# A four-layer graph network kernel: one transfer sums two neighbouring slots, a front's steps have fixed homes, 16 tile buffers, a third of the slots summed

## The chip, the core and the metric

The kernel runs on one core of a Trainium2 chip. A core has a matrix engine (PE), a vector engine (DVE), a scalar engine (ACT), a general engine (POOL), a sequencer for transfers (SP) and 16 DMA engines that they share. The time is device microseconds of one execution; lower is better.

## The reference, cut to what matters

64 batches of 256 nodes with 128 features go through four layers, each of the form x = x + layer(relu(layernorm(x))), all with one 256 x 256 matrix adj. The first three are a gated network of five steps, a polynomial in adj, and one product with adj. The last is attention over all pairs of nodes:

```python
W1, W2 = (W[:, :F], W[:, F:])                     # W is adj here
s1 = jnp.einsum('bkf,ef->bke', x, W1)
s2 = jnp.einsum('bkf,ef->bke', x, W2)
pre = s1[:, :, None, :] + s2[:, None, :, :] + b_lin
h = jnp.where(pre >= 0, pre, ALPHA * pre)         # b x 256 x 256 x 256
e = jnp.einsum('bije,e->bij', h, a) + bias
attn = jax.nn.softmax(e, axis=2)
out = jax.nn.sigmoid(jnp.einsum('bij,bjf->bif', attn, x))
```

The tensor h has 256 values for each of 64 x 256 x 256 pairs of nodes, about a thousand million in all, and each goes through a comparison and a weighted sum over the last axis. That is most of the work.

## The kernel before, in words

Batches are taken in pairs, 32 in all. For each pair a **front** (`front`, L505 on) computes layers 0 to 2 and the small operands of layer 3; then the attention scores are made in **slots**, 64 for each pair, 2048 in all. A slot stands for 8 rows i of the score matrix, four row groups by two batches (or by two halves).

The 256 features of a slot are split in two parts of 128, sorted by the sign of their weight, so that a part is one **tile** of 128 partitions x 2048 values (`t[:, g, b, :]`, 1 MiB). A tile needs only min(s1, s2) or relu(s1 - s2); the linear rest of the leaky relu is computed apart (`lin`). Part 0 is made by DVE in one instruction (L956), part 1 by ACT in eight (L964), and POOL makes either part in eight (L970). PE then **scores** the tile: `score` (L1032 on, its matmuls at L1044) multiplies it by a window of signs, so that the sum over 128 features lands in the right row of a PSUM bank.

Some slots are **joined** (`JOINED`, L896, a share of 3 in 10, not in the last 96 slots). For them POOL makes the second part in the same min form as the first, and a DMA issued from POOL adds the one tile onto the other (`add_pair`, L990, `accum_op=OP.add`). PE then scores one tile instead of two. The addend tile is free again when the transfer has landed.

There are 14 tile buffers; a producer takes the one that is free first. `MOST` (L889) bounds how many tiles of one engine may wait to be scored.

**What sets the order.** The order of the instructions on every engine is written out when the kernel is built. The loop at the end keeps a clock for each engine, and `ran` adds an assumed duration for every instruction (2.2 us for a DVE tile, 0.873 for a quarter tile of POOL, and for a transfer `ISSUE, ADDED, LANDED` at L29: time on POOL, time between two landings, time from issue to landing). Whichever engine's clock is least behind takes what is ready: the tails and fronts first, then transfers, scores and bank fills, then tiles. `part_of` decides whether POOL makes part 0, 1 or 2. So the assumed durations decide how many tiles fall to each engine; on the chip each engine runs its list in order and waits on semaphores.

A front is a chain of steps in fixed order (`yield engine, since`), paced so that it is finished when its pair's slots come up. Its intermediate tensors (h, mT, rh, d, hT, x1, x2 ...) come from rotating pools: one pool of 12 buffers (`SHORT`), one of 4 for hT, one of 3 for x1 and x2. The first pair's two batches run apart (`alone`) and borrow two tile buffers each. The normalisation in a front uses small POOL operations (L408, L409, L489) between DVE's statistics and ACT's activation (L493). Inputs, the rows for the tail and the outputs are moved by SP's queue.

Of the kernel before, what the change touches and what calls it, by code (L numbers as in the profile page):

```python
# [8 lines left out]
F32 = mybir.dt.float32  # L9
AF = mybir.ActivationFunctionType  # L10
OP = mybir.AluOpType
# [13 lines left out]
SHARE = (3, 10)  # L25
# [3 lines left out]
ISSUE, ADDED, LANDED, SLACK = 0.93, 5.9, 7.0, 0.3  # L29
# [3 lines left out]
def kernel(  # L33
# [65 lines left out]
    tiles = [[relu_pool.tile([P, 4, NB, N], F32, name=f"rl{k}", bufs=1), 0.0] for k in range(14)]  # L99
    scratch = tiles[0][0].rearrange("p g b n -> p (g b n)")  # L100
# [60 lines left out]
    def load_x(p):  # L161
        if p >= NPAIR:
            return
        XIN[p] = work.tile([P, NB, NC, D], F32, name="xin", bufs=2)
        for b in range(NB):
            nc.sync.dma_start(XIN[p][:, b], x[p * NB + b].rearrange("(c p) d -> p c d", p=P))
# [6 lines left out]
    place = scratch[:, 0:N].bitcast(mybir.dt.int32)  # L173
# [9 lines left out]
    def load_raw(w):  # L183
        raw = work.tile([P, 2 * D], F32, name="w_raw", tag="short", bufs=12)
        nc.sync.dma_start(raw[:, :w.shape[1]], w)
        return raw
# [6 lines left out]
    th_raw = scratch[:, N:N + 5 * D].rearrange("p (k o) -> p k o", k=5)  # L193
# [36 lines left out]
    def first_constants():  # L230

        for c in range(NC):
            yield PE, 6.0, 1
            b = take()
            for k in range(NC):
                nc.tensor.transpose(b[0][:, k * P:(k + 1) * P], adj_n[:, k, c * P:(c + 1) * P], ident)
            t = ran(PE, 0.4, 6.0, b[1])
            yield DVE, t
            nc.vector.tensor_copy(adj_t[:, c, :], b[0][:, 0:N])
            t = ran(DVE, 0.35, t)  # L240
            spare.append([b[0], t])
        SET_UP.add("adj")
        sums = [raws[0][:, :D]]
        yield DVE, 6.5
        for raw in raws[1:4]:
            sums.append(work.tile([P, D], F32, name="w_sum", tag="short", bufs=12))
            nc.vector.tensor_add(sums[-1], raw[:, :D], raw[:, D:])
        t = ran(DVE, 0.6, 6.5)
        yield PE, t, 1
        b = take()  # L250
        for k, src in enumerate(sums):
            nc.tensor.transpose(b[0][:, k * P:(k + 1) * P], src, ident)
        t = ran(PE, 0.7, t, b[1])
        yield DVE, t
        nc.vector.tensor_copy(wts[:, 0:4].rearrange("p k o -> p (k o)"), b[0])
        nc.vector.tensor_sub(w34, w3t, w4t)
        t = ran(DVE, 0.85, t)
        spare.append([b[0], t])
        yield PE, 7.0, 1
        b = take()  # L260
        nc.tensor.transpose(b[0][:, 0:P], raws[4][:, :D], ident)
        t = ran(PE, 0.25, 7.0, b[1])
        yield DVE, t
        nc.vector.tensor_scalar(u5t, b[0][:, 0:P], 0.5, None, op0=OP.mult)
        t = ran(DVE, 0.25, t)
        spare.append([b[0], t])
        nc.vector.tensor_add(gate_b[:, 0:1], braw[:, 0:1], braw[:, 3:4])
        nc.vector.tensor_add(gate_b[:, 1:2], braw[:, 1:2], braw[:, 3:4])
        nc.vector.tensor_add(gate_b[:, 2:3], braw[:, 2:3], braw[:, 4:5])
        nc.vector.tensor_scalar(gate_b[:, 0:2], gate_b[:, 0:2], 0.5, None, op0=OP.mult)  # L270
        nc.vector.tensor_scalar(bh_n, bh, -1.0, None, op0=OP.mult)
        ran(DVE, 0.3)
        SET_UP.add("first")

    def other_constants():
# [31 lines left out]
        placed = work.tile([P, N], F32, name="placed", tag="short", bufs=12)  # L307
        nc.vector.tensor_copy(placed, place)
        nc.vector.tensor_copy(number, feature)
        before = work.tile([P, P], F32, name="before", tag="short", bufs=12)  # L310
        nc.vector.tensor_scalar(before, placed[:, 0:P], number[:, 0:1], None, op0=OP.is_gt)
        ones = work.tile([P, P], F32, name="ones", tag="short", bufs=12)
# [23 lines left out]
        among = work.tile([P, P], F32, name="among", tag="short", bufs=12)  # L336
# [10 lines left out]
        moved_to = work.tile([P, NE, NE, P], F32, name="moved_to", tag="short", bufs=12)  # L347
# [3 lines left out]
        adj_s = work.tile([P, NE, N], F32, name="adj_s", tag="short", bufs=12)  # L351
# [107 lines left out]
    def feat(name, **kw):  # L459
        return work.tile([P, NB, N], F32, name=name, **kw)  # L460

    def tok(name, **kw):
        return work.tile([P, NB, NC, D], F32, name=name, **kw)
# [3 lines left out]

    SHORT = dict(tag="short", bufs=12)

# [29 lines left out]
    def front(p, batches):  # L499
# [17 lines left out]
        def feature(name, **kw):  # L517
            return part().unsqueeze(1) if alone else feat(name, **(kw or SHORT))

        def token(name, **kw):  # L520
            return part().rearrange("p (b c d) -> p b c d", b=1, c=NC) if alone else tok(name, **(kw or SHORT))

# [14 lines left out]
        def copied(name, bank, t, **kw):  # L537

            c = feature(name, **kw)
            nc.scalar.copy(c, seen(bank))  # L540
            t = ran(ACT, COPY[nb], t)
            spare.append([bank[0], t])
            return c, t
# [10 lines left out]
        hT, t_hT = copied("hT", b, t, bufs=4)  # L554
        for step in range(STEPS):
# [5 lines left out]
            mT, t_m = copied("mT", b, t)  # L561
# [25 lines left out]
            rh = feature("rh")  # L587
# [23 lines left out]
            d = feature("d")  # L611
# [18 lines left out]
            hT_new = feature("hT", bufs=4)  # L630
# [15 lines left out]
        x1 = token("x1", tag="x12", bufs=3)  # L646
# [12 lines left out]
        c1T, t_c = copied("c1T", b, t)  # L659
# [5 lines left out]
        hT, t = copied("hT", b, t, bufs=4)  # L665
# [10 lines left out]
        c2T, t = copied("c2T", b, t)  # L676
# [12 lines left out]
        x2 = token("x2", tag="x12", bufs=3)  # L689
# [18 lines left out]
        yT, t = copied("yT", b, t)  # L708
# [12 lines left out]
        sq = token("sq")  # L721
# [27 lines left out]
        hT, t_hT = copied("hT", b, t, bufs=4)  # L749
# [78 lines left out]
    def tail(u, pe, since, own=range(NB)):  # L828
# [10 lines left out]
        sc = feat("sc", **SHORT)[:, 0:nb]  # L839
# [16 lines left out]
        wT = tok("wT", **SHORT)[:, 0:nb]  # L856
# [32 lines left out]
    MOST = {DVE: 8, ACT: 3, POOL: 4}  # L889
# [6 lines left out]
    JOINED = [n for n in range(NSLOT - ALONE) if (n + 1) * SHARE[0] // SHARE[1] > n * SHARE[0] // SHARE[1]]  # L896
# [4 lines left out]
    adding = [0.0]  # L901

# [32 lines left out]

    def work_on_tile(e):
        if e not in begun:
            k = part_of(e)
            tiles.sort(key=lambda t: t[1])
            begun[e] = [slot(k), k, *tiles.pop(0), 0]  # L940
            following[k] += 1
            held[e] += 1
            if k < 2:
                READY[where(begun[e][0])[0]]["left"][k] -= 1
# [39 lines left out]
    def pair_ready():  # L984

        return min(((max(x[0] for x in both.values()), n) for n, both in pairs.items() if len(both) == 2), default=None)

    def add_pair(n):
        (since, t, e), (since_z, z, e_z) = pairs[n][0], pairs.pop(n)[2]
        nc.gpsimd.dma_start(out=t.rearrange("p g b n -> p (g b n)"), in_=z.rearrange("p g b n -> p (g b n)"), accum_op=OP.add)  # L990
        issued = ran(POOL, ISSUE, since, since_z)
        done = adding[0] = max(adding[0] + ADDED, issued + LANDED)
        held[e] -= 1
        held[e_z] -= 1
        tiles.append([z, done])
        made.append((done, n, 2, t, None))
# [179 lines left out]
```

## Time and profile before

| what | value |
|---|---|
| median of 3 runs | 4719.98 us (4719.92 to 4722.61) |
| profiled execution | 4720.04 us, span 4718.2 us |
| granted PE clock | 0.999 |
| transfers that sum tiles | 585, 1024 KB each, median 8.1 us from issue to landing |
| software queue q0 | 613.45 MB, 64.9% of the 16 DMA engines' span |
| tiles made: DVE, ACT, POOL | 1775, 1235, 1086 |

How to read it: the profile's page gives busy time by engine and the costliest groups of instructions. A group's line has the source line, engine, operation, output <- inputs, shapes, count, then busy time in us and mean duration in ns, then the idle time of the engine just before these instructions and what ended it. Instructions of PE, ACT and POOL overlap with the next of the same engine, so a mean duration is longer than the step from one start to the next. PEld is PE's loading of weights.

### The profile page before, as it was taken

The page shows a single profiled execution, that of the slowest core. Times are in us where ns is not written, and L with a number is a line of the kernel's source. Part 1 is how long each engine was busy: PE and PEld are TensorE (multiplying, and loading weights), DVE is VectorE, ACT ScalarE, POOL GpSimd, SP SyncE. Part 2 cuts the span into 40 slices and gives each one's busy share as a digit, 9 for nine tenths or more (in the row PEclk, how much of TensorE's full clock was granted, in tenths as well). Part 3 has the DMA queues.
Part 4 walks back from the last instruction along what each step waited for, and adds up shares of the span by engine and source line. Part 5 has one row for each costly group of instructions (what it writes and reads, how often), then busy time and mean ns, then how long its engine had stood idle before and what let it go on. Part 6 is the DMA issues. An engine that isn't in the chain of part 4 may idle for free.

```text
span 4718.2 us, 133077 instructions
## 1 busy us (share of the span) xinstructions
PE 4693.0 (99%) x51711; PEld 1724.1 (37%) x51711; DVE 4638.2 (98%) x3664; ACT 4615.2 (98%) x12059; POOL 4565.5 (97%) x9776
## 2 busy tenths in 40 slices
PE   9999999999999999999999999999999999999999
PEld 4333333333333333333333333333333333333332
DVE  5999999999999999999999999999999999999999
ACT  5999999999999999999999999999999999999999
POOL 2999999999999999999999999999999999999998
PEclk9999999999999999999999999999999999999999
DMA  1767777777777777777777777777777777777720
GB/s 33 148 139 153 147 144 157 145 148 147 148 150 147 142 152 149 147 147 146 150 146 148 148 151 143 150 153 150 145 144 147 149 153 144 146 145 148 153 61 5
DMA packets 129378, 656.97 MB, mean 139 GB/s; under 512 B 14696, under 2 KB 49896, under 8 KB 53864
## 3 DMA queue, kind: packets, MB, share of 16 engines
q0 software_dynamic: 84240, 613.45, 64.9%
q1 hardware_dynamic: 43784, 35.01, 2.5%
q8 instruction: 404, 6.62, 0.5%
q14 instruction: 230, 1.88, 0.1%
q10 hardware_dynamic: 720, 0.00, 0.0%
HBM read 26.48 MB, written 8.52 MB: 7 GB/s over the span
## 4 chain that ended last, share of the span: by engine, by line
PE 80%; DVE 10%; POOL 4%; issue 2%; DMA 2%; ACT 2%; SPq 0%; POOLq 0%; DVEq 0%; ACTq 0%
PE bank L1044 52%; PE bank L414 25%; DVE rl L956 8%; POOL rl L970 3%; PE bank L447 2%; DMA rl<-rl 2%; ACT rl L964 1%; PE bank L439 1%; POOL rl L990 0%; DVE bank L627 0%; DVE d L623 0%; DVE hT L631 0%; DVE rh L588 0%; DVE stats L484 0%; DVE bank L836 0%
## 5 line engine op out<-in xcount | busy, mean ns | idle before, releaser
L956 DVE TENSOR_TENSOR rl<-s1a,bank 128x2048 f32<-128x2048 f32 x1775 | 3964.5, 2277 | 8.7 <-DMA rl<-rl 4.9
L964 ACT ACTIVATE rl<-bank,s1b 128x256 f32<-128x256 f32 x9880 | 3938.3, 727 | 5.2 <-PE bank L1044 3.5
L970 POOL TENSOR_SCALAR rl<-s2n,s1b 128x256 f32<-128x256 f32 x6504 | 3101.4, 790 | 18.7 <-ACT s1b L802 7.5
L1044 PE MATMUL bank<-rl,win_n 128*32 128x512 f32 x18208 | 2258.9, 593 | 7.0 <-DMA rl<-rl 4.9
L1044 PE MATMUL bank<-rl,win 128*32 128x512 f32 x9880 | 1303.8, 593 | 0.0
L970 POOL TENSOR_SCALAR rl<-s2c,s1a 128x256 f32<-128x256 f32 x2184 | 1054.3, 741 | 2.4
L1044 PEld LDWEIGHTS bank<-rl,win_n 128*32 128x32 f32 x18208 | 586.0, 110 | 1210.5 <-issue 1022.9
L990 POOL DMA_DIRECT2D rl<-rl x585 | 617.4, 1068 | 3.8 <-DVE rl L956 1.5
L1044 PEld LDWEIGHTS bank<-rl,win 128*32 128x32 f32 x9880 | 319.9, 110 | 633.8 <-issue 509.2
L414 PE MATMUL bank<-mT,wts 128*32 128x512 f32 x2480 | 322.8, 592 | 0.0
L414 PE MATMUL bank<-adj_t,h 128*32 128x256 f32 x4960 | 297.5, 380 | 2.4 <-ACT h L642 2.4
L414 PEld LDWEIGHTS bank<-adj_t,h 128*32 128x32 f32 x4960 | 159.8, 110 | 163.0 <-issue 48.0
L493 ACT ACTIVATE h<-x,mv 128x128 f32<-128x128 f32 x376 | 166.7, 617 | 11.1 <-POOL mv L489 10.3
L414 PE MATMUL bank<-mT,w 128*32 128x512 f32 x1240 | 161.5, 592 | 0.8 <-ACT bank L584 0.8
L414 PE MATMUL bank<-hT,wts 128*32 128x512 f32 x1240 | 161.8, 593 | 0.0
L414 PE MATMUL bank<-rh,u5t 128*32 128x512 f32 x1240 | 161.4, 592 | 0.0
L584 ACT ACTIVATE bank<-bank,gate_b 128x512 f32<-128x512 f32 (+1 forms) x165 | 138.0, 836 | 20.1 <-PE bank L414 17.4
L414 PEld LDWEIGHTS bank<-mT,wts 128*32 128x32 f32 x2480 | 80.4, 110 | 185.9 <-issue 137.0
L607 ACT ACTIVATE bank<-bank,gate_b 128x512 f32<-128x512 f32 (+1 forms) x165 | 138.4, 839 | 9.7 <-PE bank L414 9.5
L409 POOL TENSOR_TENSOR mv<-mv,minus_half 128x4 f32<-128x4 f32 (+1 forms) x132 | 133.8, 1014 | 11.0
L540 ACT COPY mT<-bank 128x512 f32<-128x512 f32 x155 | 123.9, 800 | 12.7 <-PE bank L414 11.9
L620 ACT ACTIVATE bank<-bank,gate_b 128x512 f32<-128x512 f32 x155 | 131.1, 845 | 3.1 <-PE bank L414 3.1
(207 smaller groups left out, 3164.4 us busy)
## 6 DMA issues: line engine op xcount, KB each, us to landing
rl<-rl POOLq DMA_DIRECT2D x585, 1024.0 KB, 8.1
rows<-row SPq DMA_DIRECT2D x31, 512.0 KB
xin<-in_x_dram SPq DMA_DIRECT2D x64, 128.0 KB
out_dram<-o SPq DMA_DIRECT2D x63, 128.0 KB
row<-quarter SPq DMA_DIRECT2D x62, 2.0 KB
rows<-row SPq DMA_DIRECT2D x2, 256.0 KB
w_raw<-in_L_gnn_w_w_dram SPq DMA_DIRECT2D x3, 128.0 KB
rl<-in_L_gnn_Theta_dram SPq DMA_DIRECT2D x1, 320.0 KB
```

Of the source, the lines that this page charges most:

```text
L409: nc.gpsimd.tensor_tensor(t, t, minus_half[:, 0:t.shape[1]], op=OP.pow)
L414: nc.tensor.matmul(o[g:g + 32], w[:, g:g + 32], t, start=start, stop=stop, skip_group_check=True)
L493: nc.scalar.activation(h[:, k, :], s[:, k, :], AF.Relu, bias=mv[:, k, 0:1], scale=mv[:, k, 1:2])
L540: nc.scalar.copy(c, seen(bank))
L584: nc.scalar.activation(seen(r), seen(pr), AF.Tanh, bias=br, scale=0.5)
L607: nc.scalar.activation(seen(pr), seen(pr), AF.Tanh, bias=bz, scale=0.5)
L620: nc.scalar.activation(seen(pv), seen(pv), AF.Tanh, bias=bh_n, scale=-1.0)
L956: nc.vector.tensor_tensor(t, rows.to_broadcast(whole), ops["s2a"].unsqueeze(1).to_broadcast(whole), op=OP.min)
L964: nc.scalar.activation(t[:, g, b, :], other(ops["s2b"], b), AF.Relu, bias=rows[:, g, b], scale=-1.0)
L970: nc.gpsimd.tensor_scalar(t[:, part, b, :], other(ops["s2n" if k else "s2c"], b), rows[:, part, b], MOST_NEGATIVE, op0=OP.min, op1=OP.max)
L990: nc.gpsimd.dma_start(out=t.rearrange("p g b n -> p (g b n)"), in_=z.rearrange("p g b n -> p (g b n)"), accum_op=OP.add)
L1044: nc.tensor.matmul(pe[g * 32:(g + 1) * 32, :], w[:, 31 - r:63 - r], flat(t[:, g]), start=False, stop=(left[u] == 0), skip_group_check=True)
```

## The change

- `add_pair` takes one or two slots. Two neighbours (n and n + 1, n even) that are both joined are summed by one transfer of 128 x 2 x 2048 values, if the two target tiles and the two addend tiles can each be written as one strided pattern (`in_step`); if not, each slot has its own transfer. The transfer of two is issued when all four tiles are made.
- `JOINED` chooses neighbours together, and a third of the slots instead of three in ten.
- All tiles are one tensor `rl` with 16 buffers instead of 14 tensors. `chosen` picks the last buffer of a group of four so that the patterns fit.
- The front's tensors have fixed homes, `HOMES`: h, m, r and hT, one set for even and one for odd pairs. hT, x1 and x2 are computed in place. The set-up's raw weights and small matrices lie in tile buffers (`borrowed`).
- The input has three buffers instead of two; ACT may hold four tiles instead of three. The assumed durations of a transfer have a value for one slot and one for two.

```diff
-SHARE = (3, 10)
+SHARE = (1, 3)
...
-ISSUE, ADDED, LANDED, SLACK = 0.93, 5.9, 7.0, 0.3
+TILES = 16
+ISSUE, ADDED, LANDED, SLACK = (None, 0.93, 1.15), (None, 5.9, 10.6), (None, 7.0, 11.8), 0.3
...
-    tiles = [[relu_pool.tile([P, 4, NB, N], F32, name=f"rl{k}", bufs=1), 0.0] for k in range(14)]
-    scratch = tiles[0][0].rearrange("p g b n -> p (g b n)")
+    rl = relu_pool.tile([P, TILES, 4, NB, N], F32, name="rl", bufs=1)
+    tiles = [[rl[:, k], 0.0 if k > 2 else 40.0] for k in range(TILES)]
+    number = {id(t): k for k, (t, _) in enumerate(tiles)}
...
-        XIN[p] = work.tile([P, NB, NC, D], F32, name="xin", bufs=2)
+        XIN[p] = work.tile([P, NB, NC, D], F32, name="xin", bufs=3)
...
+    HOMES = [{k: work.tile([P, NB, N], F32, name=f"{k}{p}", bufs=1) for k in ("h", "m", "r", "hT")} for p in range(2)]
...
+            return part().unsqueeze(1) if alone else HOMES[p % 2][name]
...
-            rh = feature("rh")
+            rh = feature("r")
...
-            d = feature("d")
+            d = feature("r")
...
-            hT_new = feature("hT", bufs=4)
+            hT_new = feature("hT") if alone else hT
...
-        x1 = token("x1", tag="x12", bufs=3)
+        x1 = token("x1") if alone else x0
...
-        x2 = token("x2", tag="x12", bufs=3)
+        x2 = token("x2") if alone else x1
...
-    MOST = {DVE: 8, ACT: 3, POOL: 4}
+    MOST = {DVE: 8, ACT: 4, POOL: 4}
...
-    JOINED = [n for n in range(NSLOT - ALONE) if (n + 1) * SHARE[0] // SHARE[1] > n * SHARE[0] // SHARE[1]]
+    JOINED = [n for n in range(NSLOT - ALONE) if (n // 2 + 1) * SHARE[0] // SHARE[1] > n // 2 * SHARE[0] // SHARE[1]]
...
+    def chosen(n, k):
+
+        tiles.sort(key=lambda t: t[1])
+        best = tiles[0]
+        if n in WITH and k != 1:
+            group = taken.setdefault(n // 2, {})
+            if len(group) == 3:
+                best = next((t for t in tiles if t[1] <= max(tiles[0][1], min(now.values())) and
+                             in_step({**group, (n % 2, k): number[id(t[0])]})), best)
+            group[n % 2, k] = number[id(best[0])]
+        tiles.remove(best)
+        return best
+
+    def in_step(group):
+
+        t, z, t_next, z_next = (group[h, k] for h in range(2) for k in (0, 2))
+        return (t < t_next) == (z < z_next) or (t < z_next) == (z < t_next)
...
     def pair_ready():
...
+        for n, both in pairs.items():
+            whole = [n // 2 * 2, n // 2 * 2 + 1]
+            if in_step_of(n):
+                if any(len(pairs.get(m, ())) < 2 for m in whole):
+                    continue
+            else:
+                whole = [n]
...
+    def add_pair(whole):
...
+        if len(whole) == 2:
+            a, b = ([number[id(t)] for t in part] for part in parts)
+            if (a[0] < b[0]) != (a[1] < b[1]):
+                b.reverse()
+                parts[1].reverse()
+            into, of = (rl[:, min(i, j):max(i, j) + 1:abs(i - j)].rearrange("p s g b n -> p s (g b n)") for i, j in zip(a, b))
+        else:
+            into, of = (t.rearrange("p g b n -> p (g b n)") for t in parts[0])
+        nc.gpsimd.dma_start(out=into, in_=of, accum_op=OP.add, max_dma_last_dim=8192)
+        issued = ran(POOL, ISSUE[len(whole)], since)
+        done = adding[0] = max(adding[0] + ADDED[len(whole)], issued + LANDED[len(whole)])
...
```

## The prediction

> **What bounds the kernel now.** I read the busy time of each engine first, then a table of stretches, then the costliest groups, the instructions of GpSimd in order of time, the chain that ended last, and the waits. The page's first part and the table of stretches:
>
> ```profile
> PE 4693.0 (99%) x51711; PEld 1724.1 (37%) x51711; DVE 4638.2 (98%) x3664; ACT 4615.2 (98%) x12059; POOL 4565.5 (97%) x9776
> ...
> core 0: us, PE busy (x) PEld busy (x) DVE busy (x) ACT busy (x) POOL busy (x), PEclk, DMA share, GB/s
> 0.00:60.00 60.00, 53.95 (x705) 27.76 (x709) 30.38 (x104) 27.80 (x63) 4.80 (x17) 1.00 0.12 32
> 240.00:4540.00 4300.00, 4290.49 (x47352) 1568.94 (x47351) 4280.43 (x3306) 4258.56 (x11126) 4250.41 (x9076) 1.00 0.72 147
> ```
>
> Between 240 and 4540 us all four engines are full: no one engine is the bound, and work taken off one is worth something only if the other three shrink too. Busy time flatters ACT and POOL, though, because their instructions overlap. So I use the step from one start to the next. The groups:
>
> ```profile
> L956 DVE TENSOR_TENSOR rl<-s1a,bank 128x2048 f32<-128x2048 f32 x1775 | 3964.5, 2277 | 8.7 <-DMA rl<-rl 4.9
> L964 ACT ACTIVATE rl<-bank,s1b 128x256 f32<-128x256 f32 x9880 | 3938.3, 727 | 5.2 <-PE bank L1044 3.5
> L970 POOL TENSOR_SCALAR rl<-s2n,s1b 128x256 f32<-128x256 f32 x6504 | 3101.4, 790 | 18.7 <-ACT s1b L802 7.5
> L970 POOL TENSOR_SCALAR rl<-s2c,s1a 128x256 f32<-128x256 f32 x2184 | 1054.3, 741 | 2.4
> L990 POOL DMA_DIRECT2D rl<-rl x585 | 617.4, 1068 | 3.8 <-DVE rl L956 1.5
> ```
>
> A tile is one DVE instruction, eight ACT or eight POOL instructions: 1775 + 9880/8 + 8688/8 = 4096 tiles, two for each of 2048 slots. POOL in order of time, and one stretch of the chain:
>
> ```profile
> 2000.22 0.82 POOL L990 DMA_DIRECT2D rl<-rl  x1
> 2000.93 7.19 POOL L970 TENSOR_SCALAR rl<-s2n,s1b 128x256 f32<-128x256 f32 x16
> 2008.07 0.86 POOL L990 DMA_DIRECT2D rl<-rl  x1
> 2008.70 7.28 POOL L970 TENSOR_SCALAR rl<-s2n,s1b 128x256 f32<-128x256 f32 x16
> 2016.07 0.20 POOL L408 TENSOR_SCALAR mv<-stats 128x4 f32<-128x4 f32 x1
> 2016.35 1.03 POOL L409 TENSOR_TENSOR mv<-mv,minus_half 128x4 f32<-128x4 f32 x1
> ```
>
> ```profile
> 2403.74 12.02 PE bank L1044 x112
> ```
>
> Sixteen tensor_scalars take 7.19 us, 0.448 each; a transfer holds POOL not for its 1.07 us of group time but for 0.63 us to the next start (8.07 to 8.70), and since the tensor_scalar ahead of it is cut 0.03 short, it adds 0.60. The 4-element L408 steps by 0.28 (16.07 to 16.35): about what any instruction costs here. PE scores a tile (eight matmuls) in 12.02/14 = 0.859. Successive DVE tiles start 2.198 apart, ACT's instructions 0.356 apart. What each engine spends beyond those steps in the 4300 us is its true slack: DVE 39 us, ACT 154, POOL 97 (its tensor_scalars without a semaphore wait show none of it, so it is waiting). PE is idle for 9.5.
>
> **The change, part by part.** The order of instructions of both kernels is fixed when they are built, so their counts can be compared: DVE tiles 1775 to 1755, ACT's activations 9880 to 9792, POOL's tensor_scalars 8688 to 8936, scored tiles 3511 to 3446, transfers 585 to 350, of which 300 carry two slots and 50 one (25 neighbours whose buffers could not be put in step). Summed slots go from 585 to 300 x 2 + 50 = 650.
>
> - PE: 65 tiles less, x 0.859 = -56 us.
> - DVE: 20 tiles less, x 2.198 = -44 us.
> - ACT: 88 activations less, x 0.356 = -31 us, on top of a slack of 154.
> - POOL: 248 tensor_scalars more, x 0.448 = +111; 235 transfers less, x 0.60 = -141; and 300 transfers that each cost d more than a single one. Sum -30 + 300 d.
>
> The price d of the second half of a transfer is not in the trace. The floor is 0: the row could be all fixed cost. The ceiling is what of 0.60 is not the common cost of an instruction, 0.60 - 0.28 = 0.32, if describing 256 rows costs twice what 128 do. The Trainium skill speaks both ways here: "DMA: Bandwidth & Descriptors", section "Anatomy of one DMA", calls descriptor generation small, "You can emit a lot of descriptors before the incremental cost shows up" (d near 0); its section "SWDGE vs HWDGE vs iDMA" has a program on GpSimd that computes one descriptor pair per DMA op, which for 128 x 2 rows I read as twice the work (d near 0.32), and that speaks against the change. No run here shows either. Both ends have a row behind them, the middle none; I take 0.16, as far from one row as from the other.
>
> With it POOL does +18 us. Now the slacks decide. DVE: -44 with its 39 us of waits unchanged makes the middle 4256 us. POOL: 4300 - 97 = 4203 of work, + 18 = 4221, and if POOL too cannot do with less than the 39 us of waits that DVE has, 4260. So POOL ends up as full as DVE: the change is worth 40 to 44 us, not PE's 56. By the first rule (POOL -30) DVE stays ahead and it is 44, 4676 us; by the second (POOL +66, 4203 + 66 + 39 = 4308) it is 8 us worse than before, 4728.
>
> The transfer itself: 64.9% of 4718.2 us over 585 transfers is 5.23 us of all 16 DMA engines each; a single lands 8.1 us after its issue by the page's median, so a pair should land at about 8.1 + 5.2 = 13.3 (an estimate from these two). The skill's formula in the same "Anatomy" section, 2.0 us + bytes over 436 GB/s, would make a pair 6.8 us in all; the 6.7 us minimum for a single 1 MiB transfer already contradicts it, so the row counts. The queue gets busier, 650 x 5.23 = 3400 us, 72% of the span. What waits for a landing: PE's score of both slots, and the producer that gets the two addend tiles. Both are far from the path today (waits by pair: us in total, times, longest):
>
> ```profile
> PEld bank L1044 <- DMA rl<-rl: 13.2, 16, 3.5
> PE bank L1044 <- DMA rl<-rl: 4.9, 4, 2.5
> DVE rl L956 <- DMA rl<-rl: 4.9, 7, 1.1
> ```
>
> The order puts a score behind the landing that it assumes (ISSUE + LANDED, 12.95 for a pair, 7.93 before), and other scores cover it. A pair is 0.35 later than assumed, a single 0.17; the 18 us of PE's wait may double. I charge 2 us of it to the end: PE loses 56 us and can spend them.
>
> Tiles are held longer: a pair needs four, all made before the issue (up to one POOL tile, 3.6 us, longer for the first), and the landing is 5 us later. Counting buffers in the order, at each new tile 10.7 of 14 are in use before, 12.1 of 16 after: 3.3 free, then 3.9. Cost 0; if the cover were gone, every producer would wait for PE.
>
> The transfer now waits for four tiles rather than two. Behind it on POOL stand POOL's next tile and the normalisation's small operations, for which ACT's activation L493 waits, and so the chain of the next front. Today POOL waits 1.5 us for DVE there; with 350 issues instead of 585, and POOL fuller and so rather late than early, I take 0.
>
> Fixed homes, the sum in place (hT, x1, x2), three xin buffers: 0. Each new writer of a home stands in its front's own chain behind the last reader; no instruction is added. SP's load of the next pair waits for a buffer given up one pair earlier, so the row and output transfers behind it aren't held. The borrowed set-up rows lie in three tiles unused until 40 us; POOL is idle for 55 of the first 60 us: 0 to +3. The last 96 slots are unsummed in both, and PE's run from 4595.88 stays.
>
> Sum against the profiled execution, 4720.04 us (span 4718.2 and 1.8 around it; the median of the runs is 4719.98): 4720 - 40 + 2 = 4682.
>
> **The rivals.**
> POOL becomes the bound, slower: place, POOL's queue at each double issue. Break-even is where -30 + 300 d uses up 97 - 39 = 58, d = 0.29. At 0.32 4728; if a double issue cost a full two, d = 0.60, 4720 + 150 - 58 = 4812. For: POOL has little slack. Against: an instruction's common cost is paid once.
> The gain is handed back: landings later than assumed stall PE in order. 300 pairs x 0.13 us are 39: about 4719. For: the queue at 72%. Against: 18 us of such waits in 585 transfers, and PE's 56.
> Better than counted: with d near 0 POOL and ACT run ahead, half of DVE's 39 us of waits go: 4720 - 44 - 20 = 4656. PE's 56 us plus its 9.5 of idle put the floor at 4655.
> The change doing nothing is excluded for the counts, which are fixed; whether a double transfer is one issue at all is d.
>
> **How the numbers follow.** The likeliest case has 0.68 and its own range 4664 to 4704 (d from 0 to 0.24); POOL bound 0.13, handed back 0.11, better 0.08. A difference under 0.2% (9.4 us) cannot be told from none here. Faster is the first and the last case and a part of the third, 0.79; same 0.07; slower the second and a remainder, 0.14. Range 4657 to 4724: it takes in better and handed back, and leaves POOL bound and the lowest edge out.
>
> **What would show it.** Right: the transfer group x350 with POOL's next start 0.7 to 0.85 us after a double issue; landing near 13 us; DVE's group near 3920 us busy and x1755; all four engines still over 98% in the middle; POOL's slack under 60 us. Wrong: next starts at 0.9 or more, with PE and DVE waiting for POOL tiles (POOL bound); PE or DVE waits on transfers of over 40 us (handed back); waits of producers on PE's scores (buffers short).

## The result, and the profile after

The changed kernel takes 4755.91 us (median of 4 runs, 4747.57 to 4756.84) beside 4720.28 for the kernel before: 1.0071 of its time, 95% interval 1.0053 to 1.0088. It is 36 us slower where I had forecast 38 faster. The profiled execution took 4755.6 us, its span 4753.8. Waits are read from one profiled execution of each kernel, and in three of the runs further down (e0_rooms, e1_singles, e2_told_true) it took 9 to 13 us longer than the median.

Busy time, share of the span and instructions of each engine, from the first part of the page of the kernel after:

```profile
PE 4672.8 (98%) x51191; PEld 1754.6 (37%) x51191; DVE 4601.8 (97%) x3644; ACT 4588.2 (97%) x11971; POOL 4558.7 (96%) x9789
```

The stretch between 240 and 4540 us of the same execution (columns as before the change: PE, PEld, DVE, ACT, POOL, then clock, share of the DMA engines and GB/s):

```profile
240.00:4540.00 4300.00, 4236.29 (x46485) 1580.89 (x46480) 4211.82 (x3256) 4199.39 (x10952) 4207.18 (x9008) 1.00 0.88 162
```

PE, DVE and ACT have less work, as counted, and all four engines stand still more: DVE was busy for 4280 of these 4300 us and is now for 4212, PE for 4290 and now 4236. The groups of the tiles and transfers:

```profile
L985 DVE TENSOR_TENSOR rl<-s1a,bank 128x2048 f32<-128x2048 f32 x1755 | 3922.4, 2276 | 48.6 <-DMA rl<-rl 30.3
L993 ACT ACTIVATE rl<-bank,s1b 128x256 f32<-128x256 f32 x9792 | 3873.0, 688 | 28.1 <-DMA rl<-rl 24.7
L999 POOL TENSOR_SCALAR rl<-s2n,s1b 128x256 f32<-128x256 f32 x6592 | 3038.1, 646 | 48.9 <-DMA rl<-rl 22.0
...
L1103 PE MATMUL bank<-rl,win_n 128*32 128x512 f32 x17776 | 2244.3, 595 | 50.7 <-DMA rl<-rl 45.6
...
L1050 POOL DMA_DIRECT2D rl<-rl x350 | 393.3, 1137 | 5.4 <-POOL rl L999 2.4
```

The idle time before DVE's tiles went from 8.7 to 48.6 us, and for DVE, ACT and PE most of the idle time in these groups ends with a transfer, for POOL 22.0 of 48.9 us. The transfers (queue: packets, MB, share of 16 engines; issues: KB each, us to landing), then the longest waits for them (us, times, longest):

```profile
q0 software_dynamic: 88800, 681.60, 79.3%
...
rl<-rl POOLq DMA_DIRECT2D x300, 2048.0 KB, 14.5
rl<-rl POOLq DMA_DIRECT2D x50, 1024.0 KB, 12.4
```

```profile
PEld bank L1103 <- DMA rl<-rl: 100.0, 85, 3.2
...
PE bank L1103 <- DMA rl<-rl: 45.6, 46, 2.6
DVE rl L985 <- DMA rl<-rl: 30.3, 31, 2.5
ACT rl L993 <- DMA rl<-rl: 24.7, 20, 2.9
POOL rl L999 <- DMA rl<-rl: 22.0, 15, 4.7
```

That is 223 us of waits for landings, added over engines that wait in part at the same time, where there were 25. The queue took 79.3% of the DMA engines, 5.80 us for each slot (79.3% x 4753.8 / 650) instead of 5.23. In the chain that ended last, PE fell from 80% to half, and DMA rose from 2% to 17%, POOL from 4% to 14% (the kernel before, then the kernel after):

```profile
PE 80%; DVE 10%; POOL 4%; issue 2%; DMA 2%; ACT 2%; SPq 0%; POOLq 0%; DVEq 0%; ACTq 0%
...
PE 50%; DMA 17%; POOL 14%; DVE 10%; ACT 6%; issue 3%; POOLq 0%; DVEq 0%; ACTq 0%
```

A double issue on POOL, and what starts after it:

```profile
2031.73 1.06 POOL L1050 DMA_DIRECT2D rl<-rl  x1
2032.60 3.76 POOL L999 TENSOR_SCALAR rl<-s2n,s1b 128x256 f32<-128x256 f32 x8
...
2043.33 1.15 POOL L1050 DMA_DIRECT2D rl<-rl  x1
2044.13 7.40 POOL L999 TENSOR_SCALAR rl<-s2n,s1b 128x256 f32<-128x256 f32 x16
```

The next start comes 0.80 to 0.87 us after a double issue (the quarter and three-quarter marks of all are 0.80 and 0.87; a single's median was 0.63). So d, which I had set at 0.16, is about 0.19.

The waits also go with a lower clock of PE. In the middle of this execution PE waits eight times for about 2 us or more, each time for a landing, and at five of these waits the granted clock is at half for 3.4 us. One of them, the wait and then the stretch after it (columns as above):

```profile
700.00:702.00 2.00, 0.03 (x3) 0.01 (x2) 2.00 (x3) 2.00 (x6) 2.00 (x5) 1.00 0.46 78
702.40:705.60 3.20, 3.20 (x28) 1.14 (x24) 1.00 (x1) 2.45 (x7) 3.20 (x8) 0.50 0.93 164
```

The kernel before has no such stretch in the middle, the profiled executions of the runs below at most two. Five times 3.4 us at half clock are 8.5 us of PE's work, an estimate, and that is also how much the four executions differ: three, at a mean clock of 0.997, took 4755.6 to 4756.8 us, and one, at 0.999, took 4747.57. So some 8 of the lost us go with the clock. That a long wait brings the low clock is the reading; three waits as long had none, and no run tests it.

### The profile page after: what moved, and what is told of

Read it like the earlier page. It is cut to its first block, busy times and chain, and to the rows that moved or that the text cites. A ratio compares the mean times of both kernels' runs of the same rounds, so it can differ in the third digit from the quotient of the medians.

```text
span 4753.8 us, 131288 instructions
## 1 busy us (share of the span) xinstructions
PE 4672.8 (98%) x51191; PEld 1754.6 (37%) x51191; DVE 4601.8 (97%) x3644; ACT 4588.2 (97%) x11971; POOL 4558.7 (96%) x9789
## 3 DMA queue, kind: packets, MB, share of 16 engines
q0 software_dynamic: 88800, 681.60, 79.3%
## 4 chain that ended last, share of the span: by engine, by line
PE 50%; DMA 17%; POOL 14%; DVE 10%; ACT 6%; issue 3%; POOLq 0%; DVEq 0%; ACTq 0%
PE bank L1103 31%; DMA rl<-rl 17%; PE bank L429 17%; POOL rl L999 13%; DVE rl L985 8%; ACT rl L993 4%; PE bank L462 1%; POOL rl L1050 1%; PE bank L454 1%; POOL mv L424 0%; ACT h L504 0%; DVE r L634 0%; DVE bank L638 0%; DVE r L599 0%; DVE hT L642 0%
## 5 line engine op out<-in xcount | busy, mean ns | idle before, releaser
L985 DVE TENSOR_TENSOR rl<-s1a,bank 128x2048 f32<-128x2048 f32 x1755 | 3922.4, 2276 | 48.6 <-DMA rl<-rl 30.3
L993 ACT ACTIVATE rl<-bank,s1b 128x256 f32<-128x256 f32 x9792 | 3873.0, 688 | 28.1 <-DMA rl<-rl 24.7
L999 POOL TENSOR_SCALAR rl<-s2n,s1b 128x256 f32<-128x256 f32 x6592 | 3038.1, 646 | 48.9 <-DMA rl<-rl 22.0
L1050 POOL DMA_DIRECT2D rl<-rl x350 | 393.3, 1137 | 5.4 <-POOL rl L999 2.4
L429 PE MATMUL bank<-m,wts 128*32 128x512 f32 x2480 | 329.8, 592 | 0.0
L551 ACT COPY m<-bank 128x512 f32<-128x512 f32 x217 | 160.4, 739 | 28.1 <-PE bank L429 27.4
L504 ACT ACTIVATE h<-xin,mv 128x128 f32<-128x128 f32 x372 | 170.9, 687 | 3.5 <-POOL mv L500 3.5
L429 PE MATMUL bank<-m,w 128*32 128x512 f32 x1240 | 165.1, 593 | 0.8 <-ACT bank L595 0.8
L429 PE MATMUL bank<-r,u5t 128*32 128x512 f32 x1240 | 164.7, 592 | 0.0
L429 PEld LDWEIGHTS bank<-m,wts 128*32 128x32 f32 x2480 | 84.3, 110 | 182.4 <-issue 138.6
## 6 DMA issues: line engine op xcount, KB each, us to landing
rl<-rl POOLq DMA_DIRECT2D x300, 2048.0 KB, 14.5
```

Of the source, the lines that this page charges most:

```text
L429: nc.tensor.matmul(o[g:g + 32], w[:, g:g + 32], t, start=start, stop=stop, skip_group_check=True)
L504: nc.scalar.activation(h[:, k, :], s[:, k, :], AF.Relu, bias=mv[:, k, 0:1], scale=mv[:, k, 1:2])
L985: nc.vector.tensor_tensor(t, rows.to_broadcast(whole), ops["s2a"].unsqueeze(1).to_broadcast(whole), op=OP.min)
L993: nc.scalar.activation(t[:, g, b, :], other(ops["s2b"], b), AF.Relu, bias=rows[:, g, b], scale=-1.0)
L999: nc.gpsimd.tensor_scalar(t[:, part, b, :], other(ops["s2n" if k else "s2c"], b), rows[:, part, b], MOST_NEGATIVE, op0=OP.min, op1=OP.max)
L1050: nc.gpsimd.dma_start(out=into, in_=of, accum_op=OP.add, max_dma_last_dim=8192)
```

## The experiments

For each run I use one yardstick: 4720 us plus 2.2 us for every DVE tile more than 1775, what the time would be if DVE's waits were those of before. For the kernel after it gives 4720 - 44 = 4676, so 80 us are to be explained, some 8 of which go with the clock. Three theories stood at the start: LATE (a transfer of two lands later than the written-out order assumes, and the engines stand in line behind it), FULL (the DMA engines are too busy), HOMES (the homes or the common tensor add waits). A fourth, CUSHION (POOL has no slack left), came after the first runs. Further names (ROWS, CROWD, TIGHT, EDGE, EVEN) are explained in the expectation where each first stands.

**Without pairs, share of before (e0_rooms).**

```diff
     def in_step_of(n):
-        return len(taken[n // 2]) < 4 or in_step(taken[n // 2])
+        return False
...
-SHARE = (1, 3)
+SHARE = (3, 10)
```

> The kernel after with every summed slot in a transfer of its own and the share back at three in ten: fixed homes, one tensor with 16 tiles, three input buffers and neighbours chosen together stay; 584 single transfers, DVE makes 1774 tiles, 3512 tiles scored (before: 585, 1775, 3511). Theory LATE (a transfer of two lands later than the order assumes, and the engines stand in their fixed order behind it): without pairs nothing is late, 4712 to 4724 us. Theory FULL (the 16 DMA engines are too busy, 79%, whatever the order assumes): the same, 4712 to 4724. Theory HOMES (the homes or the common tensor add waits): 4745 to 4760.

4717.35 us, ratio 0.9992 (0.9983 to 1.0001); yardstick 4718. Homes, 16 tiles and the third input buffer, taken together, cost nothing and bring nothing that can be told from none: HOMES falls.

**Without pairs, share of one third (e1_singles):** the first of the two edits alone.

> The kernel after with every summed slot in a transfer of its own, 650 of them, a share of one third; DVE makes 1781 tiles (before 1775), POOL 1073 (before 1086), 3446 scored (before 3511). LATE: nothing is late, and DVE has 6 tiles, 13 us, more than before: 4725 to 4740 us. FULL: 650 x 5.23 us is 72% of the DMA engines: half of the loss, about 4735 to 4745. HOMES: over 4755.

4733.45 us, ratio 1.0031 (1.0020 to 1.0043); yardstick 4733. PE waits 69 us for landings here (52.3 for its weight loads and 16.9) and the time is still that of DVE's tiles: PE has 56 us less to do while DVE has 13 us more, and neither DVE, ACT nor POOL waits for a landing. The dearer way to sum more slots is a loss by itself: the POOL time of 650 issues pushes tiles to DVE.

**The order told what a double transfer takes (e2_told_true).**

```diff
-ISSUE, ADDED, LANDED, SLACK = (None, 0.93, 1.15), (None, 5.9, 10.6), (None, 7.0, 11.8), 0.3
+ISSUE, ADDED, LANDED, SLACK = (None, 0.93, 1.15), (None, 5.9, 12.2), (None, 7.0, 13.6), 0.3
```

> The kernel after, with the order told what a transfer of two takes: 12.2 us between landings (was 10.6) and 13.6 from issue to landing (was 11.8); 288 pairs and 74 single transfers, DVE 1756 tiles. LATE: PE's and the producers' waits on transfers fall from 223 us to under 60 and the time to 4680 to 4705 us. FULL: the DMA engines are as busy as before this edit, 4745 to 4760. HOMES: 4745 to 4760.

4723.52 us, ratio 1.0007 (1.0000 to 1.0014): 32 us better than the kernel after, but not the 4680 to 4705 of LATE. The waits on transfers fell as expected, to 45 us. FULL is refuted in this form: the DMA engines are as busy as before the edit (share 0.88 in the middle). What remains is of another kind:

```profile
ACT h L504 <- POOL mv L500: 30.1, 48, 1.8
...
PEld bank L1103 <- DMA rl<-rl: 20.8, 27, 2.1
...
DVE x L746 <- POOL rn L424: 12.1, 12, 1.6
DVE rl L985 <- DMA rl<-rl: 11.6, 11, 3.1
```

ACT and DVE wait 42 us for the small normalisation operations on POOL (12 us before the change, 10.5 of them in this line):

```profile
ACT h L493 <- POOL mv L489: 10.5, 20, 1.3
```

Such waits are a sign that POOL is late, not the loss itself: e0_rooms has 31 us of them (26.4 and 4.3) and lost nothing.

**Transfers alone (m1_transfers).** A kernel with nothing but transfers between tiles; all four layers are left out.

```diff
+    for turn in range(4):
+        for k in range(8):
+            nc.gpsimd.dma_start(out=rl[:, k], in_=rl[:, 8 + k], accum_op=OP.add, max_dma_last_dim=8192)
+        for k in range(0, 8, 2):
+            nc.gpsimd.dma_start(out=rl[:, k:k + 2], in_=rl[:, 8 + k:10 + k], accum_op=OP.add, max_dma_last_dim=8192)
...
```

> Only transfers, on an otherwise idle core (all four layers are left out and the output is not computed): four turns of eight single sums of 128 x 2048, four sums of 128 x 2 x 2048, eight sums of 128 x 2 x 1024, two sums of 128 x 4 x 2048, and plain copies of 128 x 2 x 2048 and 128 x 2048. ROWS (two packets in a row on the same partition hinder each other, so the form itself costs): a sum of two lands 11.5 to 12 us after the one before it where two singles take 9.8 to 10.5, its second packets take 0.8 us, a single cut in half rows is slower than a whole one by over 1 us, and four slots take 23 to 24. CROWD (the second packets are slow because the engines use the memory at the same time): on an idle core a sum of two takes 9.8 to 10.5 and all packets 0.65.

Four stretches of it, in which the queue is never empty: singles, doubles, singles in half rows, four slots at once (columns: DVE, POOL, clock, DMA share, GB/s):

```profile
24.00:60.00 36.00, 9.23 (x6) 8.71 (x9) 1.00 1.03 206
64.00:104.00 40.00, 0.00 (x0) 8.42 (x7) 1.00 1.02 183
108.00:148.00 40.00, 0.00 (x0) 3.69 (x3) 1.00 1.05 190
152.00:194.00 42.00, 0.00 (x0) 2.71 (x3) 1.00 1.03 174
```

By their landings a single follows a single after 5.1 us on average, a double a double after 11.4, four slots four slots after 24.2. So the form itself moves 11% fewer bytes in the same time with two rows and 16% fewer with four, on an idle core too: CROWD falls. The packets tell how: in a double, the first row of a partition takes 0.65 us as in a single, the second 0.81, in turn through the whole transfer, and the same in the kernel after; with four rows, a quarter of the packets take 0.64 and the others 0.82. Half rows, which are slower by 0.5 us where I had written over 1, fit in kind and not in size. That the second packet stands behind the first because both go to one partition is the reading; nothing but this pattern shows it.

**Shorter transfers, same order (e7_half_bytes).**

```diff
-        nc.gpsimd.dma_start(out=into, in_=of, accum_op=OP.add, max_dma_last_dim=8192)
+        nc.gpsimd.dma_start(out=into[..., 0:2 * N], in_=of[..., 0:2 * N], accum_op=OP.add, max_dma_last_dim=8192)
```

> The kernel after, its instructions in the same order on every engine, but each transfer moves half of each row (so half of every summed slot's second part is left out of the result). The issue on POOL costs the same, the landing comes about 5 us earlier. LATE and FULL (the length of the transfer is the cause, as lateness or as load): PE's and the producers' waits on transfers fall from 223 us to under 40 and the time to 4672 to 4695 us, what DVE's 1755 tiles leave (4720 - 44). CUSHION (POOL, with 248 more tensor_scalars and dearer issues, has no slack left and everything waits for it): 4715 to 4750.

4705.88 us, ratio 0.9972 (0.9962 to 0.9982): 50 of the 80 us. The edit does more than I had written. A row has 2048 values and `2 * N` is 512, so each transfer moves a quarter of each row, not half, and the landing comes much earlier (us to landing, where it was 14.5):

```profile
q0 software_dynamic: 88800, 170.42, 21.2%
...
rl<-rl POOLq DMA_DIRECT2D x300, 512.0 KB, 5.2
```

No engine waited for a transfer any more. Thirty us remain that no transfer can explain, between the two theories' figures. As both the lateness and the load are gone, this run does not tell LATE from FULL. ACT's wait for POOL is as in e2_told_true:

```profile
ACT h L504 <- POOL mv L500: 30.4, 50, 1.7
```

**Lateness alone, in the kernel before (e3_before_early).**

```diff
-ISSUE, ADDED, LANDED, SLACK = 0.93, 5.9, 7.0, 0.3
+ISSUE, ADDED, LANDED, SLACK = 0.93, 4.8, 5.4, 0.3
```

> The kernel before with an order that assumes transfers earlier than they are: 5.4 us from issue to landing instead of 7.0, 4.8 between landings instead of 5.9, so that a landing comes some 1.5 us after the order expects it, as with the pairs. Tiles and transfers as before (DVE 1776, 585 transfers). LATE: waits on transfers go from 25 us to over 100 and the time to 4735 to 4765 us. FULL and CUSHION: the work is the same, 4715 to 4726.

4745.40 us, ratio 1.0053 (1.0038 to 1.0068), with one DVE tile more; 103 us of waits on transfers. The landing came 8.2 us after the issue where this order assumes 0.93 + 5.4 = 6.3. An order that expects its landings 1.9 us early costs 25 us with no other change: LATE is shown as a mechanism, near the size that the told run gave back (32, some 8 of them the clock's). The kernel before, beside this run, took 4719 to 4723 us in all 28 executions, so the 4741 us that it took beside two later runs (at the end of this section) is no rival here.

**The order told of POOL's steps as well (e5_told_pool).**

```diff
-ISSUE, ADDED, LANDED, SLACK = (None, 0.93, 1.15), (None, 5.9, 10.6), (None, 7.0, 11.8), 0.3
+ISSUE, ADDED, LANDED, SLACK = (None, 0.60, 0.80), (None, 5.9, 12.2), (None, 7.3, 13.9), 0.3
...
-            done = ran(POOL, 0.873, since)
+            done = ran(POOL, 0.897, since)
```

> As the run that told the order of the landings (4723.5 us), and also of POOL's true steps: 0.897 us for a quarter tile (was 0.873), 0.60 us for a single and 0.80 for a double issue (were 0.93 and 1.15). DVE 1753 tiles, POOL 1120, 291 pairs. What is left of the loss is POOL's lag behind the order: the small normalisation operations of POOL no longer hold up ACT and DVE (41 us of waits before) and the time goes to 4680 to 4705. POOL is simply full (CUSHION): 4718 to 4735. FULL: 4718 to 4730.

4728.24 us, ratio 1.0017 (1.0010 to 1.0024): no gain, 5 us worse than the run told of the landings alone. With true steps POOL is given 1120 tiles, three more than in the kernel after, and stays as full as it was. A true assumption is not the point; slack is.

**POOL lightened, same order (e8_half_light, e9_light, e11_before_light).** The edit, made to the run with shorter transfers, to the kernel after, and to the kernel before:

```diff
-                nc.gpsimd.tensor_scalar(t[:, part, b, :], other(ops["s2n" if k else "s2c"], b), rows[:, part, b],
+                wide = N if (id(t), part, b) not in WHOLE else N - 32
+                WHOLE.add((id(t), part, b))
+                nc.gpsimd.tensor_scalar(t[:, part, b, 0:wide], other(ops["s2n" if k else "s2c"], b)[:, 0:wide], rows[:, part, b],
```

> As the run with half rows (4705.9 us), in the same order of instructions, and POOL's tensor_scalars write 224 of 256 columns after the first use of a tile buffer (an eighth of POOL's tiles is left out), which takes some 0.02 us off each of 8936. CUSHION (what is left of the loss, 30 us, is that POOL has no slack): ACT's wait for the normalisation on POOL falls from 30 us to under 12 and the time to 4674 to 4688. TIGHT (four equally full engines in a fixed order lose this much whatever POOL does): 4700 to 4708.

4664.73 us, ratio 0.9882 (0.9867 to 0.9897). ACT no longer waits for POOL's normalisation; POOL waits for DVE's statistics instead:

```profile
POOL mv L423 <- DVE stats L495: 144.5, 80, 37.1
```

> The kernel after with whole transfers, and POOL's tensor_scalars on 224 of 256 columns (an eighth of POOL's tiles left out). LATE as the larger part: POOL issues earlier by what it lagged, so a little of the lateness goes: 4722 to 4740. CUSHION as the larger part: under 4715. TIGHT: 4745 to 4757.

4680.74 us, ratio 0.9915 (0.9899 to 0.9932): 75 of the 80 us, with the transfers as they were:

```profile
q0 software_dynamic: 88800, 681.60, 80.0%
...
rl<-rl POOLq DMA_DIRECT2D x300, 2048.0 KB, 14.6
```

> The kernel before, with POOL's tensor_scalars on 224 of 256 columns (an eighth of POOL's tiles left out). CUSHION: before the change POOL has slack and DVE is the bound, so nothing moves, 4714 to 4721 us. If POOL's lag costs the kernel before as much as the kernel after: 4690 to 4705.

4708.11 us, ratio 0.9975 (0.9965 to 0.9985): the same lightening is worth 12 us to the kernel before, a little more than CUSHION had allowed and far from 75 (the lightening takes about 230 us off POOL).

The kernel after with transfers late, 14.6 us to the landing and 80% of the DMA engines, reaches what I had predicted for it if only POOL is lighter. FULL is dead, and LATE alone too. But POOL alone is not the cause either, since shorter transfers gave back 50 us with POOL as full as ever. Each repair alone gives most of what both give (75 and 50, together 91). A lighter POOL also repairs some of the lateness: it issues earlier, and the waits on transfers fell from 223 to 90 us with the same 14.6 us to the landing. Each cause costs something without the other: lateness alone 25 us (e3_before_early, where POOL had its slack), the full POOL alone 30 (e7_half_bytes, where nothing was late). Together they cost 80, more than the sum: a landing later than assumed, and a POOL that cannot get ahead to make up for it.

**How much slack (e12_dose48).** The edit of the lightening again, to the kernel after, with fewer columns left out:

```diff
-                wide = N if (id(t), part, b) not in WHOLE else N - 32
+                wide = N if (id(t), part, b) not in WHOLE else N - 8
```

> The kernel after with POOL's tensor_scalars on 248 of 256 columns (a thirty-second of POOL's tiles left out): some 0.005 us each, 45 to 50 us in all, about what the dearer issue of 300 double transfers costs POOL (300 x 0.19 = 57). EDGE (POOL passed the point where its slack is used up, and the first 50 us of slack are worth most): 4715 to 4730 us, half or more of the 75 us that four times as much slack gave. EVEN (each us of POOL's slack is worth the same): 4733 to 4740. LATE alone: 4745 to 4756.

4717.75 us, ratio 0.9996 (0.9987 to 1.0005). POOL's step fell from 0.448 to 0.441 us, 60 us over 8936 instructions, and the kernel gained 38: half of what some 230 us gave (0.422). The first part of the slack is worth most: EDGE. These 60 us are also the size of what the dearer double issue costs POOL, 300 x 0.19 = 57 us.

**With nothing left out (e14_told_less_pool, e15_told_mid_less_pool).** The order told of the landings, and that POOL is a little slower than it assumed, so that POOL gets fewer tiles:

```diff
-ISSUE, ADDED, LANDED, SLACK = (None, 0.93, 1.15), (None, 5.9, 10.6), (None, 7.0, 11.8), 0.3
+ISSUE, ADDED, LANDED, SLACK = (None, 0.93, 1.15), (None, 5.9, 12.2), (None, 7.0, 13.6), 0.3
...
-            done = ran(POOL, 0.873, since)
+            done = ran(POOL, 0.885, since)
```

> Nothing left out: the order told of the landings (12.2 and 13.6 us) and that a quarter tile on POOL takes 0.885 us (was 0.873), so that POOL gets 10 tiles less than in the kernel after: DVE 1761, POOL 1107, 306 pairs, 3446 scored. EDGE: POOL regains some 35 us of slack at 13 us of DVE: 4698 to 4712 us. EVEN: 4712 to 4722. LATE alone: as the run told of the landings, 4723 plus 10.

4697.69 us, ratio 0.9951 (0.9936 to 0.9966). The second run has the same edit and a smaller share of summed slots:

```diff
-SHARE = (1, 3)
+SHARE = (5, 16)
```

> Nothing left out: the same with a share of five in sixteen: DVE 1760, POOL 1109, 280 pairs and 50 single transfers, 3486 tiles scored. PE has 21 us less to do than before, DVE 33. EDGE: 4698 to 4708. EVEN: 4705 to 4712, little under the run at this share without it (4711.4).

4694.11 us, ratio 0.9944 (0.9929 to 0.9959): 26 us faster than the kernel before and 62 faster than the kernel after, the best of all kernels here that compute the whole. Its groups:

```profile
L985 DVE TENSOR_TENSOR rl<-s1a,bank 128x2048 f32<-128x2048 f32 x1760 | 3935.7, 2275 | 20.0 <-PE bank L1103 17.9
...
L1103 PE MATMUL bank<-rl,win_n 128*32 128x512 f32 x18072 | 2264.2, 593 | 1.4 <-DVE rl L985 0.8
```

Ten and eight POOL tiles fewer (1107 and 1109, against 1117) are paid with six and five DVE tiles, 13 and 11 us, and the waits shrink by far more. Five in sixteen and the order told of the landings, without the change to POOL's number (e10_told_mid):

```diff
-SHARE = (1, 3)
+SHARE = (5, 16)
...
-ISSUE, ADDED, LANDED, SLACK = (None, 0.93, 1.15), (None, 5.9, 10.6), (None, 7.0, 11.8), 0.3
+ISSUE, ADDED, LANDED, SLACK = (None, 0.93, 1.15), (None, 5.9, 12.2), (None, 7.0, 13.6), 0.3
```

> The kernel after with the order told what a transfer of two takes (12.2 and 13.6 us, as in the run with 4723.5 us) and a share of five in sixteen: 263 pairs and 84 single transfers, 3486 tiles scored, DVE 1757. LATE and CUSHION: fewer transfers are in the queue, PE has half as much to spare; 4708 to 4722 us, at best a little faster than before. FULL: DMA load falls from 79% to about 74%, 4705 to 4715.

4711.43 us, ratio 0.9981 (0.9974 to 0.9989).

**POOL's number alone (e16_less_pool, e17_less_pool_again),** landings still assumed too early, the same kernel run twice:

```diff
-            done = ran(POOL, 0.873, since)
+            done = ran(POOL, 0.885, since)
```

> The kernel after with a single number changed: the order is told that a quarter tile on POOL takes 0.885 us (was 0.873), the landings stay assumed too early. DVE 1761, POOL 1107, 295 pairs and 60 single transfers. EDGE: as the dose of 48 us (4717.8) with 13 us more for DVE and a little less slack: 4715 to 4732 us; with the run told of both (4697.7) the landings are then worth 20 to 35 us. If POOL's slack alone decides: 4695 to 4705. LATE alone: 4750 to 4765.

> The same kernel once more, on another chip: beside the last run the kernel before itself took 4741 us in 13 of 15 executions instead of 4720, so its absolute time cannot be set beside the others. By that run's ratio (0.9978) 4710 us beside a before of 4720; by EDGE with the landings still too early 4715 to 4732; if POOL's slack alone decides 4695 to 4705.

4732.29 and 4730.93 us. Beside both runs the kernel before took 4740 to 4745 us in nearly all its executions instead of 4720, on two different chips (one of which had given 4720 an hour earlier), and I don't know why; the ratio to it is 0.9978 both times (0.9968 to 0.9987, and 0.9970 to 0.9986). By that ratio the kernel would take 4710 beside a before of 4720. So telling the order of the landings is worth between 12 and 33 us on top of POOL's slack; closer than that these times do not say. In the traces, between 240 and 4540 us, DVE's steps (from one start to the next) exceed their quarter mark, the lower quartile of each kind, by 78 and 79 us there and by 47 with both, 32 us more, which speaks for the upper end, unless those executions were slowed as the kernel before was. Waits on transfers were still 138 and 143 us there, against 16 with both.

## Why the prediction was wrong, point by point

**What held.** The counts, and with them the work: DVE's group is 3922 us where I wrote near 3920. The price of the second half of a transfer: d = 0.19 where I took 0.16, between the two ends that I had, 0 and 0.32, and somewhat nearer to the second. So POOL's work grew by -30 + 300 x 0.19 = 27 us, not 18. The homes, the borrowed tiles and the input buffers at nothing (e0_rooms), the tile buffers at little: DVE's wait for PE's scores, which is where a lack of them would show, is 13 us in the kernel after (2 before), and 17 in the run that came within 7 us of the yardstick (e15_told_mid_less_pool). That DVE's tiles set the time as long as DVE does not wait: both kernels without pairs lie within 1 us of the yardstick.

**The step that failed first:** "if POOL too cannot do with less than the 39 us of waits that DVE has, 4260. So POOL ends up as full as DVE: the change is worth 40 to 44 us". I took the later of two engines, as if POOL could be filled to DVE's level at no price. POOL's slack was a cushion: POOL issues the transfers and runs the normalisation, so what it is late the others wait for. The excess of POOL's steps over their quarter mark in the middle of the run (the 97 us of slack before) is 66 to 72 us in the runs that stayed 30 to 57 us above the yardstick with few waits on transfers or none (shorter transfers 66, told of the landings 68, told of POOL too 72, five in sixteen 69), and 91 and 94 in the two that came within 9 us of it. In the kernel after this excess is 115, but there it is filled with waits for others and tells nothing; the same holds for the 92 and 93 of the two runs with POOL's number alone, 41 to 43 us above the yardstick with 138 and 143 us of waits on transfers. Lighter by 60 us, the kernel gains 38. By these runs the term should have read: POOL needs some 90 us, 2% of its time, not 39, and each us below costs the others about one to nearly three. That is an estimate from two groups of runs; no run lies between them.

**The step that failed second:** "A pair is 0.35 later than assumed ... I charge 2 us of it to the end". The landing was 14.5 us after the issue at the median and not 13.3, because the second row of each partition takes 0.81 us and not 0.65. That is 1.5 us later than the 12.95 that the order assumes. And the cover I named, PE's 56 us, does not reach far enough: a transfer that is late also holds the two addend tiles that DVE, ACT and POOL are to write next, and these waited 77 us in the kernel after. Such lateness by itself is worth about 25 us (e3_before_early) to 32 (e2_told_true, with some 8 of the clock in it), not 2.

**The rivals.** "The gain is handed back" had half of the mechanism, and the sign that I gave for it came (PE waits 46 us for transfers, its weight loads 100); I had priced it at 39 us where it was 76 to 80 with POOL's part. "POOL becomes the bound" set its break-even at d = 0.29 from the same wrong sum of slacks; with 90 us of slack to keep, 97 - 90 = 7 us are free and the break-even is d = 0.12, below what was measured. As a bound, POOL never appears in the profile of the kernel after: no engine is over 98% busy. I had given each rival its own sign, and no sign for the two together.

**The bill.** 80 us of waits above the yardstick in the kernel after. With shorter transfers 30 remain, with a lighter POOL 5. By subtraction (an account of these two repairs, both larger than the harm that they repair), of the 91 us that both give, 16 are had from the transfers only, 41 from POOL only, and 34 from either; of POOL's, 12 would be had in the kernel before as well. How the two act on each other, instruction by instruction, I have not followed.

## What to carry to other kernels

Where several engines are full at once in an order fixed beforehand, slack on the engine that hands work to the others is part of the design: count what each change leaves of it, not only who is busiest. An order written from assumed durations should be told again when a transfer changes its form, since 1.5 to 1.9 us of lateness on 300 to 600 transfers was worth 25 to 32 us. With both seen to, the same change was a gain: 4694 us, 26 less than before (e15_told_mid_less_pool). And halving the number of transfers is no gain in itself: the double one cost 1.32 times a single on its issuing engine and 2.25 times on the DMA engines.

## What the runs showed of the hardware that I had not expected

- A sum of two rows per partition is slower per byte than one: packets of 8 KB take 0.65 us for the first row and 0.81 for the second; 206 GB/s with one row, 183 with two, 174 with four (m1_transfers). It is not the addition: plain copies of two rows land 6.9 us apart where two of one row take 5.3 (2.66 each), with packets of about 0.51 and 0.32 us, half of each, against 0.32.
- A DMA issue holds POOL for far less than its group time says: 0.60 us of added time for a single (group mean 1.07), 0.79 for a double (group mean over both forms 1.14), by the next start.
- PE's granted clock fell to half for 3.4 us at five of the eight waits of about 2 us or more in the middle of the kernel after; in the kernel before, with one wait of 2.5 us, it did not. A late landing can so cost more than the wait.
